# Relative attention and routed experts on one core: the Router's turns laid out by step, and the expert blocks in program order with their layer norm behind the gates

## The chip, the cores and the metric

The kernel runs on one core of a Trainium2 chip. The metric is the device time of one execution in microseconds (us); lower is better. All times below are in us unless they say ns. The engines of a core are PE (matmul; PEld is its weight load), DVE, ACT, POOL and SP; each works through its own queue of instructions in order, and they meet through semaphores.

## The reference

```python
x = x + layernorm(attention(layernorm(x)))     # 16 x 512 x 128, 16 heads of 8
x = x + layernorm(experts(layernorm(x)))

# attention: relative keys and values, distance clipped to +-128
scores = (q @ k.T + q . rel_k[idx]) / sqrt(8)
w      = softmax(scores)
out    = w @ v + w . rel_v[idx]

# experts: 16 experts, top 1, and a shared one
logits = x @ w_router.T
e      = argmax(logits);  s = sigmoid(logits[e])
gate, up = split((s * x) @ gate_up_proj[e])
out = (up * silu(gate)) @ down_proj[e] + (silu(x @ w_gate.T) * (x @ w_up.T)) @ w_down.T
```

All data is fp32, and `layernorm` has no weights.

## The kernel before

**Attention.** There are 16 batches of 512 tokens. A batch takes 16 steps, one for each (c, n): n is the quarter of the 512 tokens and c the 32-row piece within it, so that one step handles 32 queries of all heads, in four groups g. The loop `for i in range(total + 24)` runs over 256 steps and 24 more that drain the pipeline. I write k = i % 16 for the step within a batch and n = k % 4. A step issues, in this order: `scores` of step i (`ps<-km,qb` and then `ps<-relk,qr` on PE); the transposes `pt` of step i-1; `peak` (DVE's `nmax`) and `exps` (ACT); `attend` of step i-5 (`pa` on PE, then `od`, `oz` and `oT` on DVE); the other two transposes; then at most one piece of side work called `spare`: with n = 0 `sums_turn` (`prt`), with n = 1 `output` (`py`, then `y_sb` and its statistics on DVE), with k = 6, 7, 14 and 15 the projections of the next batch. After that come POOL's `keys_advance`, the Router's turns, and with n = 1 `expand` (POOL's `qb` and `qr` for step i+3).

All engines run in the order in which the attention loop writes their instructions: the class `InOrder` wraps each engine and keeps its program order. So an instruction that waits holds up everything behind it on its engine.

**The bank.** `bank()` (L218) gives a PSUM tile from the pool `ps_o`, which has one buffer. `attend`, every `spare` and three of the Router's turns use it one after another: each must wait until the one before has been copied out.

**The Router.** `route(b)` (L595) is a generator. It takes the batch's attention output through the residual and the second layer norm, computes the logits, picks the expert, gives each token a place in a list of 128-row blocks by expert, and writes the token's row `pay` to `rows` in DRAM with an indirect DMA. Its first part runs one batch late, from step 6 of the next batch on. It is cut into sixteen turns by `yield`:

| turn | what it does |
|---|---|
| 1 | `ry` power, normalisation of y and residual (POOL) |
| 2, 3 | statistics of two pieces each (DVE) |
| 4 | `l_ve` (DVE), power `l_rs`, `x2`, the mean and 1/std into `pay` (POOL) |
| 5 | bank: transposes `ptf` of x2, copied by ACT |
| 6 | bank: logits `pl`, copied by DVE |
| 7, 8 | maximum, one-hot `oh`, score (DVE, one exponential on ACT) |
| 9 | bank: `pr`, the places within an expert; eight additions on DVE |
| 10, 11, 12 | blocks, shifts, final places `at_i` (DVE) |
| 13 to 16 | one indirect DMA each (POOL) |

In all but the last batch a step with n > 0 gives each live Router one turn. In the last batch (`nxt is None`), a small table by k says how many.

**Experts.** The second stage works on 73 blocks of 128 rows (up to 79 are possible; the rest is under a branch). `fetch` loads a block's two expert weights `gu` and `dn` by its expert number, `turn_in` normalises the rows (DVE), scales them by the Router's score (ACT) and transposes both (`ptb`), `gates` makes gate and up for the shared and the chosen expert (`pg`, 16 matmul passes), the sigmoid and two products `g` and `h`, and `leave` makes the down projection (`po`), its layer norm, adds the row and writes it out by an indirect DMA. `run` (L953) issues `turn_in(i+1)`, `gates(i)`, `leave(i-1)`. Here the engines are not wrapped: the scheduler of the framework sets the order.

Of the kernel before, what the change touches and what calls it, by code (L numbers as in the profile page):

```python
# [17 lines left out]
P = 128  # L18
# [32 lines left out]
def relative_attention_then_moe(  # L51
# [31 lines left out]
    def stats(pool, mv, src, tag, eng):  # L83
        st = pool.tile([P, 6], F32, tag=f"{tag}_st", name=f"{tag}_st")
        eng.bn_stats(st, src)
        eng.bn_aggr(mv, st)  # L86

    def own_rows(group, dma):

        tc.declare_no_dep(dma.ins, group=group, reason="rows of their own")  # L90
        tc.add_to_no_dep_group(group, dma.ins)


    with ExitStack() as actx:
# [500 lines left out]
        def route(b, c0=0, c1=NC):  # L595
# [32 lines left out]
            for t in range(nc_):  # L628
                eng.tensor_scalar(
                    x2[:, t, :], pay[:, t, 0:D], mv[:, t, 0:1], rs1[:, t : t + 1], ALU.subtract, ALU.mult  # L630
                )
            pool.tensor_copy(pay[:, :, D : D + 1], mv[:, :, 0:1])
            pool.tensor_copy(pay[:, :, D + 1 : D + 2], rs1.unsqueeze(2))
            yield
            x2T = bp.tile([P, nc_ * P], F32, tag="x2T", name=f"x2T{nm}", bufs=1)
# [122 lines left out]
        for i in range(total + 24):  # L758
            b, c, n = at(i)
            k = i % 16  # L760
            last = i - 1 if 0 <= i - 1 < total else None
            old = i - 5 if 0 <= i - 5 < total else None
            live = i < total
            done = at(i - 9)[:2] if n == 1 and 0 <= i - 9 < total else None
            nxt = b + 1 if b + 1 < B else None

            spare = None
            if 0 < b < B and k == 6:
                routes[b - 1, 0] = route(b - 1)
# [12 lines left out]
            if nxt is not None:  # L782
                if k == 0 and b + 2 < B:
                    load_x(b + 2)
                if k in (6, 7, 14, 15):
                    f = {6: x_turn, 7: queries, 14: keys, 15: values}[k]
                    spare = lambda: f(nxt)

            if live:
                scores(b, c, n)  # L790
            if last is not None:
                T = {g: turn(*at(last), g) for g in ORDER[:2]}
            if live:
                for g in ORDER[:2]:
                    peak(b, c, n, g)
                    exps(b, c, n, g)
            if last is not None:
                dve.tensor_copy(*T[ORDER[0]])
                act.copy(*T[ORDER[1]])
            if live:  # L800
                for g in ORDER[2:]:
                    peak(b, c, n, g)
                    exps(b, c, n, g)
            if old is not None:
                attend(*at(old), done=done)()
            elif done is not None:
                join_places(bank([P, P], f"pj{b}"), *done)()
            if last is not None:
                T = {g: turn(*at(last), g) for g in ORDER[2:]}
            if spare is not None:  # L810
                leave = spare()
            if last is not None:
                dve.tensor_copy(*T[ORDER[2]])
                act.copy(*T[ORDER[3]])
            if spare is not None:
                leave()
            if nxt is not None and k in (0, 2):
# [12 lines left out]

            for r in sorted(routes):


                turns = (n > 0) if nxt is not None else {7: 2, 9: 0, 12: 0, 13: 2, 15: 2}.get(k, 1) if live else 1
                for _ in range(turns):
                    bank_user = next(routes[r], StopIteration)
                    if bank_user is StopIteration:
                        del routes[r]
                        break
                    elif bank_user is not None:  # L840
                        bank_user()()
            if n == 1 and i + 3 < total:
                expand(*at(i + 3)[:2])
# [4 lines left out]
    with ExitStack() as fctx:  # L848
        wp = fctx.enter_context(tc.tile_pool(name="ffn_w", bufs=1))
        xp = fctx.enter_context(tc.tile_pool(name="ffn_x", bufs=1))  # L850
        ep = fctx.enter_context(tc.tile_pool(name="ffn_e", bufs=4))
        fp = fctx.enter_context(tc.tile_pool(name="ffn", bufs=3))
        sp = fctx.enter_context(tc.tile_pool(name="ffn_small", bufs=4))
        ps_g = fctx.enter_context(tc.tile_pool(name="ps_g", bufs=2, space=PSUM))
        ps_x = fctx.enter_context(tc.tile_pool(name="ps_x", bufs=2, space=PSUM))
        ps_f = fctx.enter_context(tc.tile_pool(name="ps_f", bufs=2, space=PSUM))

        wgu = wp.tile([P, 2 * FF], F32, name="wgu")
        wd = wp.tile([P, 2, D], F32, name="wd")
# [41 lines left out]
            st["fetched"] = last.ins  # L901
            st[i] = {"x": x, "gu": gu, "dn": dn}

        def turn_in(i):

            x = st[i]["x"]
            x2 = fp.tile([P, 2, D], F32, tag="x2", name=f"x2b{i}")
            nc.vector.tensor_scalar(
                x2[:, 0, :], x[:, 0:D], x[:, D : D + 1], x[:, D + 1 : D + 2], ALU.subtract, ALU.mult
            )  # L910
            nc.scalar.mul(x2[:, 1, :], x2[:, 0, :], x[:, D + 2 : D + 3])  # L911
            pt = ps_x.tile([P, 2, P], F32, tag="x", name=f"ptb{i}")
            for k in range(2):
                nc.tensor.transpose(pt[:, k, :], x2[:, k, :], ident)
            xT = fp.tile([P, 2, P], F32, tag="xT", name=f"xTb{i}")
            nc.scalar.copy(xT, pt)
            st[i]["xT"] = xT

        def gates(i):

            xT = st[i]["xT"]
            pg = ps_g.tile([P, 2, 4, P], F32, tag="g", name=f"pg{i}")
            for k, w in enumerate((wgu, st[i]["gu"])):
                for c in range(4):
                    nc.tensor.matmul(pg[:, k, c, :], w[:, c * P : (c + 1) * P], xT[:, k, :], start=True, stop=True)
            g = fp.tile([P, 2, 2, P], F32, tag="g", name=f"g{i}")
            nc.scalar.activation(g, pg[:, :, 0:2, :], AF.Sigmoid)
            nc.vector.tensor_mul(g, g, pg[:, :, 0:2, :])
            h = fp.tile([P, 2, 2, P], F32, tag="h", name=f"h{i}")
            nc.vector.tensor_mul(h, g, pg[:, :, 2:4, :])  # L930
            st[i]["h"] = h

        def leave(i):

            s = st.pop(i)
            x, h = s["x"], s["h"]
            po = ps_f.tile([P, D], F32, tag="f", name=f"po{i}")
            for k, w in enumerate((wd, s["dn"])):
                for c in range(2):
                    nc.tensor.matmul(po, h[:, k, c, :], w[:, c, :], start=(k == c == 0), stop=(k == c == 1))  # L940
            mv = sp.tile([P, 1, 2], F32, tag="mvf", name=f"mvf{i}")
            stats(sp, mv[:, 0, :], po, "lf", nc.vector)
            rs = rstd_of(sp, mv, 1, "lf", nc.vector)
            f = fp.tile([P, D], F32, tag="f", name=f"f{i}")
            nc.vector.tensor_scalar(f, po, mv[:, 0, 0:1], rs, ALU.subtract, ALU.mult)
            nc.gpsimd.tensor_add(f, f, x[:, 0:D])
            to = ids_of[i]
            own_rows("out", nc.gpsimd.indirect_dma_start(  # L948
                out_rows, bass.IndirectOffsetOnAxis(ap=to, axis=0), f, None,
                bounds_check=B * S - 1, oob_is_err=False,  # L950
            ))

        def run(i0, i1):  # L953

            for i in range(i0, min(i0 + 3, i1)):
                fetch(i)
            turn_in(i0)
            for i in range(i0, i1 + 1):
                if i + 3 < i1:
                    fetch(i + 3)  # L960
                if i + 1 < i1:
                    turn_in(i + 1)
                if i < i1:
                    gates(i)
                if i > i0:
                    leave(i - 1)

        for c in range(2):
            fetch_rows(c)
# [37 lines left out]
```

## Time and profile before

| | us |
|---|---|
| median of 3 runs | 1970.33 (1968.71 to 1974.59) |
| the profiled execution | 1970.49 |
| its span, first to last instruction | 1968.8 |
| outside the span | 1.69 |
| start of the first and of the last of the 256 attention steps | 23.4 and 1681.1 of the span |
| start of the first and of the last of the 73 blocks' gates | 1732.9 and 1953.4 of the span |
| granted PE clock, mean | 0.990 (about 0.5 from 1709 to 1736 and from 1958 on) |

The profile comes from one execution. Line L47 stands for every wrapped instruction, because `InOrder` records them there; such rows are told apart by their tiles, written out<-in. A timeline row has the start within the span, the duration, the engine, the line, the operation, the tiles, the shapes, how many rows were merged, and in brackets the idle time of the engine ahead of it and what ended it. "issue" there means that the profile shows nothing that the engine waited for. In a row of busy times by stretch come the stretch, its length, the busy time and count of PE, PEld, DVE, ACT and POOL, the granted PE clock, the share in which the DMA engines were busy, and GB/s.

### The profile page before, as it was taken

How to read it: one execution, taken by the hardware profiler on the slowest of the kernel's cores; microseconds unless marked ns; L12 is line 12 of the kernel's file. 1: busy time of each engine (PE TensorE's matmuls, PEld its weight loads, DVE VectorE, ACT ScalarE, POOL GpSimd, SP SyncE). 2: the span in 40 equal slices, each digit the busy share in tenths (PEclk: the TensorE clock that was granted, in tenths of full speed). 3: DMA queues.
4: the chain of work that ended last, by engine and by line, in shares of the span. 5: the costliest groups of instructions: out<-in, count | busy, mean ns of one | idle time of the engine just before them, and what ended most of it. 6: DMA issues, size and time to landing. Idle time of an engine off the chain costs nothing. (4 is left out here: it accounts for less than half of the span.)

```text
span 1968.8 us, 87947 instructions
## 1 busy us (share of the span) xinstructions
PE 1885.2 (96%) x38254; PEld 1395.1 (71%) x38254; DVE 1532.0 (78%) x4051; ACT 1146.4 (58%) x2931; POOL 1009.3 (51%) x1405
## 2 busy tenths in 40 slices
PE   6999999999999999999999999999999999689997
PEld 3667767676776767767676767677676767579997
DVE  4777787878787878787887878787878787767776
ACT  3656666666666666656566666565666666234432
POOL 4245464545454554546454645454545544246666
PEclk9999999999999999999999999999999999889998
DMA  2412000000000000000000000000000000065553
GB/s 76 75 23 52 4 23 5 18 10 11 17 5 23 5 23 3 25 3 25 3 25 3 25 3 23 4 14 14 5 18 5 18 6 6 9 181 171 177 166 95
DMA packets 88326, 68.63 MB, mean 35 GB/s; under 512 B 26439, under 2 KB 74340, under 8 KB 87808
## 3 DMA queue, kind: packets, MB, share of 16 engines
q1 hardware_dynamic: 81248, 53.60, 10.2%
q0 software_dynamic: 4384, 8.57, 1.3%
q8 instruction: 301, 4.93, 1.0%
q10 hardware_dynamic: 2304, 0.80, 0.2%
q14 instruction: 89, 0.73, 0.1%
HBM read 44.79 MB, written 18.75 MB: 32 GB/s over the span
## 5 line engine op out<-in xcount | busy, mean ns | idle before, releaser
L47 ACT ACTIVATE w<-ps,nmax 128x512 f32<-128x512 f32 x1024 | 699.0, 693 | 589.2 <-DVE nmax L47 588.6
L47 DVE TENSOR_REDUCE nmax<-ps 128x1 f32<-128x512 f32 x1024 | 655.3, 682 | 265.3 <-PE ps L47 263.8
L47 PE MATMUL pt<-ident,w 128*128 128x128 f32 x4096 | 567.7, 280 | 6.8 <-DVE wT L47 2.7
L47 PEld LDWEIGHTS pt<-ident,w 128*128 128x128 f32 x4096 | 439.2, 141 | 135.8 <-issue 89.1
L47 DVE COPY wT<-pt 128x512 f32<-128x512 f32 x512 | 348.7, 681 | 0.7 <-PE pt L47 0.7
L47 ACT COPY wT<-pt 128x512 f32<-128x512 f32 x512 | 301.1, 588 | 27.7 <-PE pt L47 27.7
L47 PE MATMUL ps<-km,qb 32*128 32x512 f32 x2048 | 297.4, 643 | 3.5 <-POOL qb L47 3.5
L47 PEld LDWEIGHTS ps<-relk,qr 64*32 64x32 f32 x8192 | 124.3, 106 | 225.8 <-issue 183.3
L47 PE MATMUL pa<-wT,v 128*32 128x128 f32 x8192 | 276.7, 276 | 2.5 <-DVE oz L47 1.4
L47 PE MATMUL ps<-relk,qr 64*32 64x288 f32 (+4 forms) x8192 | 274.8, 377 | 0.0
L47 PEld LDWEIGHTS pa<-wT,v 128*32 128x32 f32 x8192 | 208.1, 109 | 45.3 <-issue 37.8
L47 ACT ACTIVATION_READ_ACCUMULATOR w<-ps,nmax 128x1 f32 x1024 | 211.5, 207 | 0.0
L47 POOL TENSOR_TENSOR Rh<-R,mh 128x512 f32<-128x512 f32 x64 | 66.5, 1039 | 278.6 <-ACT R L47 278.6
L47 PE MATMUL pa<-wT,relv 128*32 128x48 f32 (+1 forms) x12288 | 197.1, 210 | 7.4 <-issue 7.2
L47 PEld LDWEIGHTS pa<-wT,relv 128*32 128x32 f32 x12288 | 186.2, 110 | 9.9 <-issue 9.8
L47 POOL TENSOR_TENSOR qr<-qz,mq 128x1024 f32<-128x1024 f32 x64 | 137.5, 2149 | 0.0
L47 PEld LDWEIGHTS ps<-km,qb 32*128 32x128 f32 x2048 | 82.9, 183 | 59.7 <-issue 36.3
L47 POOL COPY km<-kT 128x32 f32<-128x32 f32 (+3 forms) x207 | 53.5, 263 | 134.4 <-ACT kT L47 134.3
L47 POOL TENSOR_SCALAR km<-kT,kend 128x32 f32<-128x32 f32 (+2 forms) x223 | 115.7, 520 | 2.2 <-PE ps L47 2.2
L911 ACT ACTIVATE x2b<-x2b,xc 128x128 f32<-128x128 f32 x73 | 29.0, 401 | 125.8 <-DVE mvf L86 59.6
L47 DVE TENSOR_TENSOR od<-pa,Rh 128x128 f32<-128x128 f32 x256 | 72.9, 285 | 33.7 <-PE pa L47 30.9
L47 DVE TENSOR_REDUCE oT<-od 128x32 f32<-128x128 f32 x256 | 94.8, 370 | 0.0
(161 smaller groups left out, 2300.6 us busy)
## 6 DMA issues: line engine op xcount, KB each, us to landing
gu<-_L_ffn_gate_up_proj_dram SPq DMA_DIRECT2D x73, 256.0 KB
dn<-in_L_ffn_down_proj_dram SPq DMA_DIRECT2D x73, 128.0 KB
rows<-zero SPq DMA_DIRECT2D x19, 266.0 KB
xc<-rows SPq DMA_DIRECT2D x8, 532.0 KB
x_sb<-in_L_attn_x_dram SPq DMA_DIRECT2D x64, 64.0 KB
qd<-qp SPq DMA_DIRECT2D x16, 256.0 KB
qz<-qd SPq DMA_DIRECT2D x248, 16.0 KB
relv<-vext SPq DMA_DIRECT2D x1, 1536.0 KB
```

The source lines that it names most:

```text
L47: return lambda *a, **k: self.tc.keep_in_program_order(op(*a, **k))
L911: nc.scalar.mul(x2[:, 1, :], x2[:, 0, :], x[:, D + 2 : D + 3])
```

## The change

It has two parts.

1. *Router.* For the Routers of batches 0 to 13, the turns come at fixed steps counted from step 6 of the next batch: at offsets 0 to 7 (steps 6 to 13), 12 to 17 (steps 2 to 7 of the batch after) and 19 to 21 (steps 9 to 11). The transposes of x2 are then in step 10, the logits in step 11 and the places in step 2. Before, they were in steps 11, 13 and 1. The Routers of the last two batches keep the table by k. In turn 4 the copy of the mean into `pay` becomes one DVE operation that writes -mean x 1/std instead.
2. *Experts.* All four engines are wrapped in `InOrder`. The row's normalisation goes from DVE to ACT (it uses the -mean x 1/std from `pay`) and is issued two blocks ahead (`norm`). The gate half of `pg` is made before the up half. The products come in their own part (`product`), the down projection two blocks behind the gates (`down_proj`), and the end four blocks behind: POOL makes mean x 1/std (`mr`), ACT makes `xb` = mr - x (`residual`), and DVE makes po x 1/std - xb in one operation (`leave`), where DVE normalised and POOL added before. The buffers of the weights go from 4 to 6, of the other SBUF tiles from 3 to 4, of `ps_x` from 2 to 1, of `ps_f` from 2 to 3.

```diff
-            pool.tensor_copy(pay[:, :, D : D + 1], mv[:, :, 0:1])
+            dve.scalar_tensor_tensor(
+                pay[:, :, D : D + 1], mv[:, :, 0:1], -1.0, rs1.unsqueeze(2), ALU.mult, ALU.mult
+            )
             pool.tensor_copy(pay[:, :, D + 1 : D + 2], rs1.unsqueeze(2))
...
-                turns = (n > 0) if nxt is not None else {7: 2, 9: 0, 12: 0, 13: 2, 15: 2}.get(k, 1) if live else 1
+                if r[0] < B - 2:
+                    turns = i - (r[0] + 1) * 16 - 6 in (0, 1, 2, 3, 4, 5, 6, 7, 12, 13, 14, 15, 16, 17, 19, 20, 21)
+                else:
+                    turns = {7: 2, 9: 0, 12: 0, 13: 2, 15: 2}.get(k, 1) if live else 1
...
-        ep = fctx.enter_context(tc.tile_pool(name="ffn_e", bufs=4))
-        fp = fctx.enter_context(tc.tile_pool(name="ffn", bufs=3))
+        ep = fctx.enter_context(tc.tile_pool(name="ffn_e", bufs=6))
+        fp = fctx.enter_context(tc.tile_pool(name="ffn", bufs=4))
...
+        pe, act, dve, pool = (InOrder(tc, e) for e in (nc.tensor, nc.scalar, nc.vector, nc.gpsimd))
...
+        def norm(i):
+            act.activation(x2[:, 0, :], x[:, 0:D], AF.Identity, bias=x[:, D : D + 1], scale=x[:, D + 1 : D + 2])
+            act.mul(x2[:, 1, :], x2[:, 0, :], x[:, D + 2 : D + 3])
...
+            pg = ps_g.tile([P, 2, 2, 2, P], F32, tag="g", name=f"pg{i}")
+            for u in range(2):
+                for k, w in enumerate((wgu, st[i]["gu"])):
+                    for c in range(2):
+                        a = u * FF + c * P
+                        pe.matmul(pg[:, u, k, c, :], w[:, a : a + P], xT[:, k, :], start=True, stop=True)
...
+            act.activation(g, pg[:, 0], AF.Sigmoid)
...
+        def product(i):
+            dve.tensor_mul(g, g, pg[:, 0])
+            dve.tensor_mul(h, g, pg[:, 1])
...
+        def down_proj(i):
+            stats(sp, mv[:, 0, :], po, "lf", dve)
+            rs = rstd_of(sp, mv, 1, "lf", dve, pool)
+            pool.tensor_mul(mr, mv[:, :, 0], rs)
...
+        def residual(i):
+            act.activation(xb, s["x"][:, 0:D], AF.Identity, bias=s["mr"], scale=-1.0)
...
+            dve.scalar_tensor_tensor(f, s["po"], s["rs"], s["xb"], ALU.mult, ALU.subtract)
...
+            norm(i0)
+            norm(i0 + 1)
             turn_in(i0)
-            for i in range(i0, i1 + 1):
+            for i in range(i0, i1 + 4):
                 if i + 3 < i1:
                     fetch(i + 3)
                 if i + 1 < i1:
                     turn_in(i + 1)
+                if i + 2 < i1:
+                    norm(i + 2)
+                if i0 <= i - 4 < i1:
+                    residual(i - 4)
                 if i < i1:
                     gates(i)
-                if i > i0:
-                    leave(i - 1)
+                if i0 <= i - 4 < i1:
+                    leave(i - 4)
+                if i < i1:
+                    product(i)
+                if i0 <= i - 2 < i1:
+                    down_proj(i - 2)
```

More of the change, by code (lines that the diff above doesn't have):

```diff
@@ L850, in relative_attention_then_moe @@
         xp = fctx.enter_context(tc.tile_pool(name="ffn_x", bufs=1))
-        ep = fctx.enter_context(tc.tile_pool(name="ffn_e", bufs=4))
-        fp = fctx.enter_context(tc.tile_pool(name="ffn", bufs=3))
+        ep = fctx.enter_context(tc.tile_pool(name="ffn_e", bufs=6))
+        fp = fctx.enter_context(tc.tile_pool(name="ffn", bufs=4))
         sp = fctx.enter_context(tc.tile_pool(name="ffn_small", bufs=4))
         ps_g = fctx.enter_context(tc.tile_pool(name="ps_g", bufs=2, space=PSUM))
-        ps_x = fctx.enter_context(tc.tile_pool(name="ps_x", bufs=2, space=PSUM))
-        ps_f = fctx.enter_context(tc.tile_pool(name="ps_f", bufs=2, space=PSUM))
+        ps_x = fctx.enter_context(tc.tile_pool(name="ps_x", bufs=1, space=PSUM))
+        ps_f = fctx.enter_context(tc.tile_pool(name="ps_f", bufs=3, space=PSUM))
+        pe, act, dve, pool = (InOrder(tc, e) for e in (nc.tensor, nc.scalar, nc.vector, nc.gpsimd))
         wgu = wp.tile([P, 2 * FF], F32, name="wgu")
@@ L902, in fetch, with turn_in @@
             st[i] = {"x": x, "gu": gu, "dn": dn}
-        def turn_in(i):
+        def norm(i):
             x = st[i]["x"]
             x2 = fp.tile([P, 2, D], F32, tag="x2", name=f"x2b{i}")
[L908 to L911, printed above, removed]
+            act.activation(x2[:, 0, :], x[:, 0:D], AF.Identity, bias=x[:, D : D + 1], scale=x[:, D + 1 : D + 2])
+            act.mul(x2[:, 1, :], x2[:, 0, :], x[:, D + 2 : D + 3])
+            st[i]["x2"] = x2
+        def turn_in(i):
             pt = ps_x.tile([P, 2, P], F32, tag="x", name=f"ptb{i}")
             for k in range(2):
-                nc.tensor.transpose(pt[:, k, :], x2[:, k, :], ident)
+                pe.transpose(pt[:, k, :], st[i]["x2"][:, k, :], ident)
             xT = fp.tile([P, 2, P], F32, tag="xT", name=f"xTb{i}")
-            nc.scalar.copy(xT, pt)
+            act.copy(xT, pt)
             st[i]["xT"] = xT
@@ L921, in gates @@
             xT = st[i]["xT"]
[L922 to L925, printed above, removed]
-            g = fp.tile([P, 2, 2, P], F32, tag="g", name=f"g{i}")
-            nc.scalar.activation(g, pg[:, :, 0:2, :], AF.Sigmoid)
-            nc.vector.tensor_mul(g, g, pg[:, :, 0:2, :])
+            pg = ps_g.tile([P, 2, 2, 2, P], F32, tag="g", name=f"pg{i}")
[4 more added lines that the diff above has]
+                        pe.matmul(pg[:, u, k, c, :], w[:, a : a + P], xT[:, k, :], start=True, stop=True)
+            g = fp.tile([P, 2, 2, P], F32, tag="g", name=f"g{i}")
+            act.activation(g, pg[:, 0], AF.Sigmoid)
+            st[i].update(pg=pg, g=g)
+        def product(i):
+            pg, g = st[i]["pg"], st[i]["g"]
+            dve.tensor_mul(g, g, pg[:, 0])
             h = fp.tile([P, 2, 2, P], F32, tag="h", name=f"h{i}")
-            nc.vector.tensor_mul(h, g, pg[:, :, 2:4, :])
+            dve.tensor_mul(h, g, pg[:, 1])
             st[i]["h"] = h
-        def leave(i):
-            s = st.pop(i)
-            x, h = s["x"], s["h"]
+        def down_proj(i):
+            s = st[i]
+            h = s["h"]
             po = ps_f.tile([P, D], F32, tag="f", name=f"po{i}")
@@ L939, in leave @@
                 for c in range(2):
-                    nc.tensor.matmul(po, h[:, k, c, :], w[:, c, :], start=(k == c == 0), stop=(k == c == 1))
+                    pe.matmul(po, h[:, k, c, :], w[:, c, :], start=(k == c == 0), stop=(k == c == 1))
             mv = sp.tile([P, 1, 2], F32, tag="mvf", name=f"mvf{i}")
-            stats(sp, mv[:, 0, :], po, "lf", nc.vector)
-            rs = rstd_of(sp, mv, 1, "lf", nc.vector)
-            f = fp.tile([P, D], F32, tag="f", name=f"f{i}")
[L945 to L949, printed above, removed]
+            stats(sp, mv[:, 0, :], po, "lf", dve)
+            s["po"] = po
+            rs = rstd_of(sp, mv, 1, "lf", dve, pool)
+            mr = sp.tile([P, 1], F32, tag="mr", name=f"mr{i}")
+            pool.tensor_mul(mr, mv[:, :, 0], rs)
+            s.update(rs=rs, mr=mr)
+        def residual(i):
+            s = st[i]
+            xb = fp.tile([P, D], F32, tag="xb", name=f"xb{i}")
+            act.activation(xb, s["x"][:, 0:D], AF.Identity, bias=s["mr"], scale=-1.0)
+            s["xb"] = xb
+        def leave(i):
+            s = st.pop(i)
+            f = fp.tile([P, D], F32, tag="f", name=f"f{i}")
+            dve.scalar_tensor_tensor(f, s["po"], s["rs"], s["xb"], ALU.mult, ALU.subtract)
+            own_rows("out", pool.indirect_dma_start(
+                out_rows, bass.IndirectOffsetOnAxis(ap=ids_of[i], axis=0), f, None,
                 bounds_check=B * S - 1, oob_is_err=False,
```

## The prediction, made before the result

> **What bounds the kernel now.** I read the page's busy times first, then the busy times by stretch, then the timeline of each engine; a share over the whole span hides that the attention and the expert stage wait for different things.
>
> ```profile
> PE 1885.2 (96%) x38254; PEld 1395.1 (71%) x38254; DVE 1532.0 (78%) x4051; ACT 1146.4 (58%) x2931; POOL 1009.3 (51%) x1405
> ```
> PE has work nearly all the time, so only what makes PE wait can be won, and work merely moved on PE wins nothing. In the timeline the score matmuls `ps<-km,qb` mark the start of each step (step k = i % 16 of a batch, n = k % 4). From one to the next I take each step's length. Batches 2 to 14 repeat within 0.1 us but for a few steps.
>
> The bank `ps_o` has one buffer. Here is PE in step 13 of batch 4 (n = 1), with `py` of `output` and then the Router's logits `pl`:
> ```profile
> 519.06 1.14 PE L47 MATMUL ps<-km,qb 32*128 32x512 f32 x8
> ...
> 525.41 0.39 PE L47 MATMUL py<-wo_h,oj 128*128 128x128 f32 x2
> 526.18 1.06 PE L47 MATMUL pl<-wr,x2T 128*128 128x16 f32 x8 [0.38 <-DVE y_sb L47]
> 527.18 1.14 PE L47 MATMUL ps<-km,qb 32*128 32x512 f32 x8
> ```
> The step lasts 8.12; the same step without a Router's user (step 1 of batch 15, 1591.53 to 1598.20) lasts 6.67. Of the 1.45, 1.00 is the logits' own work and 0.45 is waiting for the bank to be emptied by DVE. Next, steps 0 and 1 of the following batch:
> ```profile
> 540.29 1.14 PE L47 MATMUL ps<-km,qb 32*128 32x512 f32 x8
> ...
> 545.65 0.66 PE L47 MATMUL pt<-ident,w 128*128 128x128 f32 x4 [0.17 <-ACT wT L47]
> 546.51 0.63 PE L47 MATMUL prt<-ident,rb 128*128 128x128 f32 x4 [0.20 <-DVE oz L47]
> 547.07 1.14 PE L47 MATMUL ps<-km,qb 32*128 32x512 f32 x8
> ...
> 554.19 0.43 PE L47 MATMUL pr<-oh,before 128*128 128x64 f32 x2 [0.39 <-DVE y_sb L47]
> ```
> Step 0 lasts 6.78 and waits for a DVE that is late; in batch 1, with no Router ahead of it, it lasts 6.12. What makes DVE late is five small Router operations after step 15, two of them slow:
> ```profile
> 541.25 0.73 DVE L47 TENSOR_TENSOR oh<-oh,km 128x64 f32<-128x64 f32 x1
> 541.90 0.71 DVE L47 TENSOR_SCALAR pay<-km 128x4 int32<-128x4 f32 x1
> ```
> Step 1 lasts 7.71: 6.67, 0.59 of `pr` work and 0.45 of waiting.
>
> In the expert stage a block takes 26 matmuls. PE starts them 0.111 apart, so 2.90 is the least, and early blocks have it; most take 3.02:
> ```profile
> 1852.49 0.67 DVE L930 TENSOR_TENSOR h<-g,pg 128x512 f32<-128x512 f32 x1
> ```
> ```profile
> 1853.21 0.71 PE L940 MATMUL po<-wd,h 128*128 128x128 f32 x4
> ...
> 1856.26 0.71 PE L940 MATMUL po<-wd,h 128*128 128x128 f32 x4
> ```
> `h` ends at 1853.16 and the down projection starts at 1853.21: it waits each time, and one POOL stall of 2.91 before an indirect DMA (1894.50) passes through DVE's queue to PE in full, 2.34.
>
> **The change, part by part.** All in us, against the profiled execution's own 1970.49 (span 1968.8 and 1.69 around it; the median shown is 1970.33, so the sum holds for that as well).
>
> *Router, batches 0 to 13.* Of the sixteen turns of a batch, numbers 3 to 11 come at other steps (the two programs, listed engine by engine, show it); the first two and the last five stay. The logits go from step 13 to 11, where n = 3 has no other user: the 1.00 of work moves, the wait of 0.45 goes, 14 times: -6.3. The places go from step 1 to 2: -0.45 x 13 = -5.9 (the fourteenth is in the last batch, below). There the bank is empty (560.20) before PE gets there (560.45), so no new wait. The five operations after step 15 now follow step 13, where POOL has just ended `qr` (525.68); behind the 0.75 of `y_sb` they end 1.9 into step 14, whose first `nmax` can start at 1.94 (529.12 - 527.18). So step 0 falls to batch 1's 6.12, -0.66 x 13 = -8.6. The operations after step 2 shorten by 0.2 (eight that read PSUM, 0.97, for 1.23 of scans and subtractions): step 3 goes from 5.92 to 5.72 as in batch 1, -2.6; step 4 keeps its 0.32 over batch 1, step 5 has 1.71 of idle DVE for what follows step 4.
>
> *Last batch.* It now follows the same list for Router 13. Step 0, 8.26, falls to 6.12; the 0.59 of `pr` stays: -1.55. Step 5, 8.62, has two indirect DMAs (1619.10, 1620.61) beside PE's densest instructions and two "issue" gaps of 0.4 there and 0.27 behind them; the DMAs move to later steps: to 6.67, -1.95. One comes to step 9, which costs 0.45 in the other batches: +0.45. Together -3.05.
>
> *Transposes of x2, step 11 to 10.* Here n = 2 is tight. The work of 0.45 moves. The `rstd` and x2 move from step 10 to 9, with the new DVE product behind them: DVE's `l_ve` can run at 502.0, POOL's power takes 1.05 and x2 3.13:
> ```profile
> 507.91 1.05 POOL L47 TENSOR_TENSOR l_rs<-l_ve,mhalf 128x4 f32<-128x4 f32 x1 [4.08 <-DVE l_ve L47]
> 509.07 3.13 POOL L47 TENSOR_SCALAR x<-pay,mv,l_rs 128x128 f32<-128x128 f32 x4
> ```
> So the power ends at 503.3 and x2 at 506.6, just before PE is free for it (506.77). The new wait on DVE, for the power, has the four `nmax` of step 10 queued behind it, and ACT's exponentials behind them; PE has the first two ready only at 503.38, so with 0.17 for the product DVE loses 0.12. It then empties the bank at 507.0, and with 0.15 of handover (as `prt` at 546.51 after `oz`) PE starts at 507.13: +0.36 x 14 = +5.0. Bounds: 0 if DVE catches up, 1.0 if the product takes 0.78 (below).
>
> *POOL behind it.* `expand` (3.5) and the key advance (0.6) of step 9 are queued behind x2, and so end at 510.7 in place of 502.6; step 12 needs them at 512.9. The indirect DMA of step 10 moves from 502.76 to 510.9, and may meet PE's dense part in step 11. Such a meeting cost 0.4 in step 9; 0 or 0.4 x 13 = 5.2, I take the middle: +2.6.
>
> *The copy of the mean* leaves POOL (0.18): hidden, POOL was idle 4.08 there. In the tail the product runs twice in DVE's waits (0.65 for `pr`): nothing, at most +0.3. Attention: -6.3 - 5.9 - 8.6 - 2.6 - 3.05 + 5.0 + 2.6 = -18.9.
>
> *Experts.* `down_proj` comes two blocks behind the gates, so `h` is ready about 1.5 before PE asks. DVE loses the normalisation (0.49) and keeps 2 x 0.675 + 0.29 + 0.17 + 0.15 + 0.41 = 2.37; ACT gets three operations of 0.40 beside 0.58 and 0.37: 2.15; POOL loses the addition (0.43) and gains a product of 128x1 (about 0.18, as its smallest copy): 1.03 + 0.3 + 0.57 + 0.18 = 2.1. All stay under 2.90, and PE sets the pace; what `f` newly waits for, ACT's `xb`, was made possible two blocks earlier. The 72 periods last 220.5 (1732.88 to 1953.36); 72 x 2.90 = 208.8. I keep the first, slow-clocked block's 0.8 and 0.7 of small gaps: -10.2. POOL's stall is then covered by a two-block lag. With six weight buffers SP may fetch one block earlier; it issues a block in 1.8. At the start ACT does both halves of two blocks before it copies `xT` (+0.5), and the gate half needs the first `gu` after 4 matmuls, not 8 (+0.4): +0.9. At the end the last down projection follows the start of the last gates by 4.05 (gates 1.78, sigmoid 0.6, two products 1.37, handovers 0.3), not 4.82 (1953.36 to 1958.18), and PE stays fast (8 x 0.1), less one hop POOL to ACT: -1.6. Experts: -10.9.
>
> **Sum:** -18.9 - 10.9 = -29.8, that is 1940.7, say **1941**.
>
> **Rivals.** *DVE is held by POOL.* The slow rows above (0.73, 0.71) run beside POOL's `v` additions and end with them; alone such rows take 0.22 and 0.16. The new product reads two SBUF tiles just when POOL's x2 begins, 0.78 apiece: if x2 comes first, +0.6 x 14 = 8.4. The Router's additions after step 4 stand 0.2 ahead of POOL's `Rh` and `Rz` (1.04 each); if they fall behind, DVE is 1.1 late, of which 0.27 is idle time: +0.83 x 13 = 10.8. So 1949 with the first and 1960 with both. For the forecast speaks that after a power DVE begins 0.03 later (1961.52 + 0.58, then 1962.14) and POOL 0.11.
> The Trainium skill, "SBUF — State Buffer", section "Who interferes with whom", says that a DVE instruction with two SBUF inputs contends with a GpSimd instruction that reads SBUF, and that the second to issue blocks until the first finishes. The trace agrees: all of the `oh<-oh,km` beside the `v` additions take 0.73.
>
> *ACT becomes the experts' bound.* Five operations with a handover of 0.2 each would be 3.15 a block, above 3.02; its queue now has the sigmoid behind the norms. Then the 10.2 is lost: 1951. Against it: where work stands ready, ACT's rows follow without a gap (0.40 at 1850.67, the sigmoid at 1850.98).
>
> *The Router's moves cancel on PE* and only the experts gain: 1960.
>
> *Slower:* `expand` comes too late for step 12. It has 2.8 in hand after x2; PE then loses 14 us for each us beyond, and the gain is used up at 29.8 / 14 = 2.1 more, so from 4.9 late on. At 6 late it would be 1986. Only a POOL that starts the power that much later could do it, and it is free from 498.6.
>
> **Chances.** Forecast 0.58, DVE held 0.2, ACT 0.1, cancelled 0.06, slower 0.06. Below 1931 PE would need savings that I see in no row; the upper end takes in both held cases nearly: 1931 to 1959. A measurement tells 0.3% (6 us) from no change: faster by that 0.89, within it 0.05, slower 0.06.
>
> **What would show it.** Step 13 at 6.7, step 1 at 6.7, step 0 at 6.1, steps 10 and 11 at 6.6 and 6.5; the product at 0.17, not 0.8; `po<-wd,h` every 2.90 with no wait for `h`. Wrong if step 12 waits for `qr`, if step 5 exceeds 6.8, or if the sigmoid waits for ACT itself.

## The result and the profile after

| | before | after |
|---|---|---|
| median, same chip | 1970.47 | 1937.57 (1935.27 to 1939.64, 4 runs) |
| ratio, 95% interval | | 0.9835 (0.9823 to 0.9846) |
| the profiled execution | 1970.49 | 1937.03, span 1935.3 |
| first to last attention step | 1657.7 | 1632.8 |
| last attention step to first gates | 51.8 | 52.7 |
| first gates to last gates | 220.5 | 209.3 |
| last gates to the end of the span | 15.4 | 17.0 |

It is faster by 1.65%; the forecast was 1941. The profiled executions differ by 33.5, of which the attention gives 24.9 and the experts 8.7 (the first step starts 0.1 later). PE's busy time on the page falls by 17.6; the rest of the gain is idle time that went. ACT takes over work from DVE and POOL:

```profile
PE 1867.6 (96%) x38254; PEld 1391.1 (72%) x38254; DVE 1528.0 (79%) x3995; ACT 1208.7 (62%) x3077; POOL 992.1 (51%) x1388
```

I took the length of every step again, as the distance from one `ps<-km,qb` to the next. The medians of batches 2 to 13:

| step | 0 | 1 | 2 | 3 | 4 | 9 | 10 | 11 | 13 | all 16 |
|---|---|---|---|---|---|---|---|---|---|---|
| before | 6.78 | 7.71 | 5.82 | 5.92 | 6.26 | 7.12 | 5.82 | 5.97 | 8.12 | 104.27 |
| after | 6.15 | 6.67 | 6.22 | 5.71 | 6.13 | 7.13 | 6.43 | 6.74 | 6.67 | 102.58 |

The seven steps left out are equal to 0.01. In the timeline of PE after, here are the ends of step 13 (batch 4) and of step 2 (batch 5), where the Router's bank users stood and where the places stand now:

```profile
518.73 0.39 PE L47 MATMUL py<-wo_h,oj 128*128 128x128 f32 x2
519.04 1.14 PE L47 MATMUL ps<-km,qb 32*128 32x512 f32 x8
...
550.68 0.33 PE L47 MATMUL pr<-oh,before 128*128 128x64 f32 x2
550.85 0.39 PE L47 MATMUL pr<-oh,every 128*128 128x64 f32 x2
551.16 0.71 PE L47 MATMUL ps<-km,qb 32*128 32x512 f32 x4
```

After `py` the next step follows at once, with no Router's user between. `pr` in step 2 starts without a wait (no bracket). DVE after step 13 runs the operations that were slow before at their short times:

```profile
520.13 0.23 DVE L47 TENSOR_TENSOR oh<-oh,km 128x64 f32<-128x64 f32 x1
520.27 0.17 DVE L47 TENSOR_SCALAR pay<-km 128x4 int32<-128x4 f32 x1
```

In step 11 the logits do not wait for the bank, but PE stands in the dense part ahead of them. An indirect DMA on POOL begins at 605.19, and at 606.17 PE waits for "issue":

```profile
606.34 0.63 PE L47 MATMUL pa<-wT,relv 128*32 128x48 f32 x33 [0.17 <-issue]
...
607.84 0.96 PE L47 MATMUL pl<-wr,x2T 128*128 128x16 f32 x8
608.73 1.14 PE L47 MATMUL ps<-km,qb 32*128 32x512 f32 x8
```

In the expert stage the first two distances between gates are 4.15 and 2.48; all that follow are 2.90 but the last (2.68). `h` of one block is done at 1853.02 (1852.33 + 0.69), and the down projection that follows at 1853.68 is that of the block before, so PE never waits for `h`:

```profile
1852.33 0.69 DVE L47 TENSOR_TENSOR h<-g,pg 128x512 f32<-128x512 f32 x1
```
```profile
1853.68 0.61 PE L47 MATMUL po<-wd,h 128*128 128x128 f32 x4
...
1856.58 0.61 PE L47 MATMUL po<-wd,h 128*128 128x128 f32 x4
```

Two places got worse. The first is step 9 of the last batch: 9.40 after, 6.67 before, and step 10 behind it 7.29 for 6.26. The timelines of POOL, DVE and PE there:

```profile
1614.83 1.04 POOL L47 TENSOR_TENSOR Rh<-R,mh 128x512 f32<-128x512 f32 x1 [4.25 <-ACT R L47]
1615.82 1.04 POOL L47 TENSOR_TENSOR Rz<-R,mz 128x512 f32<-128x512 f32 x1
...
1617.19 1.05 POOL L47 TENSOR_TENSOR l_rs<-l_ve,mhalf 128x4 f32<-128x4 f32 x1
```
```profile
1618.27 0.17 DVE L47 SCALAR_TENSOR_TENSOR pay<-mv,l_rs 128x4 f32<-128x4 f32 x1 [4.12 <-POOL l_rs L47]
```
```profile
1620.29 0.66 PE L47 MATMUL pt<-ident,w 128*128 128x128 f32 x4 [1.30 <-DVE wT L47]
...
1623.29 2.09 PE L47 MATMUL ps<-km,qb 32*128 32x512 f32 x8
```

The small product stands in DVE's queue ahead of the step's `nmax` and waits for POOL's power, and the power waits behind `Rh` and `Rz`. DVE begins the `nmax` at 1618.35 only, and PE stands idle for 1.30 behind it. Then its granted clock falls to 0.5 for 3.41, so that the next eight score matmuls take 2.09 for 1.14. The second place is the end, taken up below.

### The profile page after: what moved, and what is told of

It reads as the page before. It is cut to its first block, busy times and chain, and to the rows that moved or that the text cites. A ratio compares the mean times of both kernels' runs of the same rounds, so it can differ in the third digit from the quotient of the medians.

```text
span 1935.3 us, 88211 instructions
## 1 busy us (share of the span) xinstructions
PE 1867.6 (96%) x38254; PEld 1391.1 (72%) x38254; DVE 1528.0 (79%) x3995; ACT 1208.7 (62%) x3077; POOL 992.1 (51%) x1388
## 5 line engine op out<-in xcount | busy, mean ns | idle before, releaser
L47 PE MATMUL pt<-ident,w 128*128 128x128 f32 x4096 | 561.5, 280 | 4.6 <-DVE wT L47 4.0
L47 POOL DMA_INDIRECT out_dram<-f,to x73 | 75.9, 1040 | 46.1 <-issue 32.3
L47 POOL COPY rb<-rt 128x512 f32<-128x512 f32 x64 | 39.4, 616 | 114.9 <-DVE rt L47 114.7
```

Of the source, the lines that this page charges most:

```text
L47: return lambda *a, **k: self.tc.keep_in_program_order(op(*a, **k))
```

## The experiments

The runs were made on further chips, each beside the kernel before: chip B (before 1961.20), C (1975.62) and D (1961.9). A is the chip of the result (1970.47). Times of different chips cannot be compared; ratios and steps can. The changed kernel itself ran on A and C alone.

### One part at a time

e1 has the old expert stage, only with the norm's two operations fitted to the new content of `pay`; e2 has the old turns.

```diff
# e2, from the changed kernel
-                if r[0] < B - 2:
-                    turns = i - (r[0] + 1) * 16 - 6 in (0, 1, 2, 3, 4, 5, 6, 7, 12, ...)
-                else:
-                    turns = {7: 2, 9: 0, 12: 0, 13: 2, 15: 2}.get(k, 1) if live else 1
+                turns = (n > 0) if nxt is not None else {7: 2, 9: 0, ...}.get(k, 1) if live else 1
```

> The Router's part alone (the turns by step and the product on DVE), with the expert stage as before; only the two operations of the expert stage's normalisation are swapped, because the row now holds -mean/std. Theory: the steps of the changed kernel's trace are all of the attention's gain, and they do not depend on the experts: first to last step falls from 1657.7 to 1632.8, so 1970.5 - 24.9 = 1945.6, with the last batch's step 9 at 9.4 and step 11 of the steady batches at 6.74. Rival: the shares are as in the forecast, and the attention alone gives 18.9: 1951.6.

> The experts' part alone: the changed kernel with the Router's turns as before. Theory: the expert stage gives 8.7 (start +1.0, 72 periods -11.2, end +1.5), less what DVE's product at the old places costs: 1961.8, with the product waiting for POOL's power and the last batch's steps as before but for that. Batch 0, in which no Router runs, is 102.2 as before if its 2.8 came from the Router's order of instructions, and 99.4 if it came from anything else of the change. Rival: forecast's shares, 10.9: 1959.6.

Chip B. e1: 1933.39, ratio 0.9858 (0.9843 to 0.9874), -27.8. e2: 1954.15, ratio 0.9961 (0.9948 to 0.9975), -7.1. The split is that of the trace: the Router's part does most of it. Its 27.8 is more than the 24.9 of the trace. Two differences between the steps go that way: step 11 is 6.38 in e1, without the gap that it has on chip A (6.74), and the last batch is 96.44 in place of 97.87. e2 has the expert stage of the changed kernel (209.4 from first to last gates, end 17.0), and its step 9 of the last batch is 8.88, so the product alone brings that wait, 2.2. In e1 that step is 8.88 too, at the full clock; on chip A, with the fallen clock, it is 9.40.

Two things were not expected. Batch 0, where no Router runs, is 99.75 in e1 and 99.95 in e2, which has before's order of turns; over all runs here it lies between 99.0 and 104.6. So the 2.8 that batch 0 gave in the result is scatter, and no effect of the change. And step 9 is 6.67 in both, in all of batches 1 to 14 but one each, where its median is 7.12 on chip A. Its indirect DMA is there, at the same 3.54 of the step, and PE does not stop for it.

### The product later, for all and for one

```diff
# e3 (e8: the same for b == B - 2 alone)
-            dve.scalar_tensor_tensor(pay[:, :, D : D + 1], mv[:, :, 0:1], -1.0, ...)
             pool.tensor_copy(pay[:, :, D + 1 : D + 2], rs1.unsqueeze(2))
             yield
+            dve.scalar_tensor_tensor(pay[:, :, D : D + 1], mv[:, :, 0:1], -1.0, ...)
             x2T = ...
```

> The changed kernel with the product -mean/std one turn later in the program, in the turn that turns x2. Theory: only in the last batch did DVE wait for it (4.12 at 1618.27, because POOL's power stands behind Rh and Rz there): step 9 falls from 9.40 to 6.67 and step 10 from 7.29 to 6.26, TensorE's clock stays at 1.0 there, the steady batches do not move: 1937.6 - 3.8 = 1933.8. Rival: the transposes or POOL's order make that wait anyway, and the step stays over 9: 1937.6.

e3 on chip B: 1930.20, ratio 0.9841 (0.9828 to 0.9855). The last batch did as expected (step 9 6.67, step 10 6.26). The steady batches did not stay: step 10 fell from 6.43 to 6.26, but step 11 is 7.23, where e1 on the same chip has 6.38, so a batch is 0.67 longer. DVE and POOL in step 11 of e3:

```profile
600.23 2.76 DVE L47 SCALAR_TENSOR_TENSOR pay<-mv,l_rs 128x4 f32<-128x4 f32 x1
```
```profile
599.49 1.32 POOL L47 TENSOR_TENSOR qb<-qp,mh 128x512 f32<-128x512 f32 x1
600.78 2.14 POOL L47 TENSOR_TENSOR qr<-qz,mq 128x1024 f32<-128x1024 f32 x1
```

An operation on 4 numbers a partition lasts 2.76: it starts beside `qb` and ends with `qr`, at 602.92. Thirteen of the products are held in this way (2.75 to 2.77). That is the rival "DVE is held by POOL" of the prediction, at another place. In the changed kernel the product takes 0.17 each time: there it stands directly behind the power, and starts 0.07 ahead of POOL's x2 (597.73 and 597.80). The rule cited in the prediction (the Trainium skill, "SBUF — State Buffer", section "Who interferes with whom") has the second to issue blocked until the first finishes; the thirteen agree in part: DVE is blocked, but beyond `qb`, which issued first, until `qr` ends. In batch 1 of the same run the product was let go with `qb` (0.54), and in e5, below, each of two DVE operations ends with one POOL operation. What decides between the two cases was not found.

> The changed kernel with the product -mean/std one turn later for batch 14's Router alone, the one that runs in the last batch; all others stay where the power of POOL has just ended. Theory: DVE's wait in the last batch's step 9 goes (9.40 or 8.9 to 6.67) and no product is held, as 2.76 each was with all of them later: 3.3 less than the changed kernel beside it (2.2 from step 9, up to 1.1 from step 10 where the clock fell). Rival: as in the run with all products later, the product meets POOL's qb and qr and gives 2 back.

e8 on chip C: 1937.49, ratio 0.9822 (0.9803 to 0.9840), beside the changed kernel itself at 1941.97 (below). Step 9 of the last batch is 6.67 for 9.39, step 10 6.86 for 7.29: 3.2 less, where 3.3 was expected. The steps show this, not the times: the intervals of the two ratios overlap, and batch 0 with its scatter alone differs by 3.7 between the profiled executions (100.9 for 104.6). No product is held (0.155 to 0.169 each).

### The bank and DVE's small operations

```diff
# e4                                               # e5
-  ... 6, 7, 12, 13, ...                           -  ... 6, 7, 12, 13, ...
+  ... 6, 7, 11, 13, ...                           +  ... 6, 9, 12, 13, ...
```

> The changed kernel with one bank user put back: the places behind step 1, where y_sb holds the only bank, in place of step 2. Theory: step 1 goes from 6.67 to 7.71 and step 2 from 6.22 to 5.82: 0.64 a batch, 13 or 14 times, +8.6: 1946.2. Of the 0.64, 0.45 is the wait for the bank and 0.19 is pr's own work, which is longer when PE starts it from a standstill. Rival: the bank costs nothing, and the gain of steps 0 to 4 comes from DVE's small operations alone: within 1 of 1937.6.

> The changed kernel with the five small operations that make the router's key (oh, km, pay) put back from the end of step 13 to the end of step 15, where POOL adds v. Theory: oh<-oh,km and the one after it take 0.73 and 0.71 there, because POOL's v additions hold them, DVE is late for step 0, and step 0 goes from 6.14 to 6.78: 0.64 x 13 = +8.3 on the changed kernel's time of the same chip (1938 to 1942 on two chips, 1928 on the third). Rival: step 0 was late for the logits' wait in step 13, which is gone; then step 0 stays at 6.14 and the time does not move.

e4 on chip B: 1932.31, ratio 0.9846 (0.9833 to 0.9860). Step 1 is 7.71 and step 2 5.82, as expected to the hundredth. PE waits for the bank again, in each of the 14 batches:

```profile
547.13 0.43 PE L47 MATMUL pr<-oh,before 128*128 128x64 f32 x2 [0.38 <-DVE y_sb L47]
```

Step 4 falls to 6.01, which I had not expected, so that a batch is 0.53 longer than in e1 (102.26 for 101.73) and not 0.64. So the bank has its price, and the rival has fallen. The time of e4 says nothing more, as the changed kernel did not run on chip B.

e5 on chip D: 1932.79, ratio 0.9857 (0.9842 to 0.9872). Step 0 is 6.77 or 6.78 in each of batches 2 to 15, and the median of no other step moves against e9 on the same chip. DVE and POOL of e5 at the end of step 15:

```profile
531.78 0.74 DVE L47 TENSOR_TENSOR oh<-oh,km 128x64 f32<-128x64 f32 x1
532.44 0.71 DVE L47 TENSOR_SCALAR pay<-km 128x4 int32<-128x4 f32 x1
```
```profile
531.70 0.74 POOL L47 TENSOR_TENSOR v<-v,v_lo 128x256 f32<-128x256 f32 x1 [4.98 <-DVE v L47]
532.39 0.73 POOL L47 TENSOR_TENSOR v<-v,v_hi 128x256 f32<-128x256 f32 x1
```

Each is as long as the POOL operation beside it. So step 0's 0.64 comes from the five operations behind step 15, of which these two are held, and the rival (the logits' wait in step 13) has fallen: step 13 is 6.67 in e5. No run puts the logits themselves back. That they lengthened step 13 by 1.45 is read from the trace alone: without them it is 6.67, after and in batch 15 before.

### What carries the expert stage

The forecast put the period of 2.90 down to the down projection's second block of lag. e6 takes one block away from everything behind the gates, e9 only from the residual and the end, e7 leaves the order to the scheduler.

```diff
# e6: down_proj(i - 2) -> (i - 1), residual(i - 4) and leave(i - 4) -> (i - 3)
# e9:                              residual(i - 4) and leave(i - 4) -> (i - 3)
# e7
-        pe, act, dve, pool = (InOrder(tc, e) for e in (nc.tensor, nc.scalar, nc.vector, nc.gpsimd))
+        pe, act, dve, pool = nc.tensor, nc.scalar, nc.vector, nc.gpsimd
```

> The changed kernel once more, beside the runs below, because the kernel before took 1970.5 on one chip and 1961.2 on another. Theory: what differs between chips are the gaps of 0.45 in step 9 (both kernels) and 0.36 in step 11 (changed kernel only) beside an indirect DMA; where they are absent, step 9 is 6.67, step 11 is 6.38, the kernel takes some 10 less (1927 to 1929), and the ratio is a little better than 0.9835, by 4.7 of 1961, so 0.981. Rival: the gaps belong to the program, they come back here, and the ratio is 0.9835 on every chip.

> The changed kernel with the down projection one block behind the gates in place of two, and the residual and the leaving three in place of four. Theory of the forecast: the second block of lag is what hides h, so the period goes back from 2.90 to about 3.02, and the kernel loses 0.12 x 72 = 8.6. Rival, from the changed kernel's trace: h is ready 4.03 after its gates start, since the sigmoid now begins after half of the matmuls and DVE has lost the normalisation, and PE asks for it at 4.68; so the period stays at 2.90, and the tail, which POOL drains at 2.52 a block, gets one block shorter: 1 to 2.5 less than the changed kernel beside it.

> The changed kernel with the experts' engines taken without the fixed program order, so that the scheduler places the operations; PE's order stays the same, DVE gets f ahead of lf_ve and the statistics between the two products, ACT gets the norms in another order. Theory: the lag of two blocks is enough, and the time is within 2 of the changed kernel beside it. Rival: f ahead of lf_ve waits for POOL as before, the chain h to PE is late again, the period is 3.0 and the time 7 to 10 more.

> The changed kernel with residual and leaving three blocks behind the gates in place of four, the down projection still two behind: one block between mr and the residual that reads it, in place of two. Theory: what holds the period at 2.90 is that distance. With one block, ACT's xb stands in front of the sigmoid and waits for mr; the circle sigmoid 0.60, g and h 1.4, statistics and lf_ve 0.6, POOL's power and mr 1.0, xb 0.4 and some 0.1 of handovers is 4.1 long and takes a block's time: +1.2 x 72 = +86 on the changed kernel's time. Rival: mr of the block comes early enough, as only POOL's part of 1.1 lies between lf_ve and xb, and the period stays at 2.90 with a tail one block shorter: -2.5.

| | chip | median | ratio, 95% | typical period | first to last gates | from there to the end |
|---|---|---|---|---|---|---|
| changed again | C | 1941.97 | 0.9834 (0.9817 to 0.9850) | 2.90 | 209.3 | 17.0 |
| e6 | C | 1939.34 | 0.9824 (0.9809 to 0.9840) | 2.90 | 210.2 | 14.5 |
| e7 | C | 1954.74 | 0.9897 (0.9879 to 0.9915) | 3.02 | 219.5 | 19.0 |
| e9 | D | 1996.82 | 1.0172 (1.0156 to 1.0188) | 3.90 | 277.3 | 21.5 |

The changed kernel repeats its ratio on chip C, and its steps 9 and 11 (7.14 and 6.76) as on A. e6 shows that the second block of lag is not what hides `h`: the period stays. What it does hide, wholly, is one stall of POOL, 3.19 ahead of the 50th block's DMA, which all versions have (2.91 before). In the changed kernel it costs nothing, in e6 one period is 3.46, before it was 5.50. POOL in e6:

```profile
1870.39 1.09 POOL L47 DMA_INDIRECT out_dram<-f,to  x1 [3.19 <-ACT xTb L47]
```

e7 has the same lags in the program and the same matmuls in the same order, but for one early down projection, and is back at before's 3.02. The rival had the period right, and its reason only in part: `f` does stand ahead of `lf_ve`, but it waits for ACT's `xb`, and PE has no wait for `h` (none from 1760 to 1860). ACT, DVE, POOL and PE in e7:

```profile
1851.92 0.40 ACT L969 ACTIVATE xb<-xc,mr 128x128 f32<-128x128 f32 x1 [1.05 <-POOL mr L962]
1852.23 0.35 ACT L925 COPY xTb<-ptb 128x256 f32<-128x256 f32 x1
```
```profile
1852.39 0.32 DVE L976 SCALAR_TENSOR_TENSOR f<-po,lf_rs,xb 128x128 f32<-128x128 f32 x1
1852.63 0.15 DVE L78 TENSOR_SCALAR lf_ve<-mvf 128x1 f32<-128x1 f32 x1
```
```profile
1853.00 1.07 POOL L977 DMA_INDIRECT out_dram<-f,to  x1 [0.95 <-ACT x2b L915]
1854.10 0.58 POOL L80 TENSOR_TENSOR lf_rs<-lf_ve,mhalf 128x1 f32<-128x1 f32 x1
1854.76 0.19 POOL L962 TENSOR_TENSOR mr<-mvf,lf_rs 128x1 f32<-128x1 f32 x1
```
```profile
1852.64 0.44 PE L923 MATMUL ptb<-ident,x2b 128*128 128x128 f32 x2
```

In e7 `xb` runs as soon as `mr` is there, so `xb`, `f`, the DMA, the power and `mr` follow one another, and the next `xb` is at 1854.99: a circle of 3.07 (3.02 in the block before) that each block goes through once. PE seems to meet it at `ptb`, for which `ps_x` now has one buffer: ACT's copy `xTb` behind `xb` empties it at 1852.58, and the next `ptb` starts at 1852.64. e9 makes a circle by hand, and puts the products into it. ACT in e9:

```profile
1853.79 0.40 ACT L47 ACTIVATE xb<-xc,mr 128x128 f32<-128x128 f32 x1 [1.93 <-POOL mr L47]
1854.10 0.58 ACT L47 ACTIVATE g<-pg 128x512 f32<-128x512 f32 x1
```

`xb` stands ahead of the sigmoid in the queue and waits for `mr` in each block, then come the sigmoid, `g`, `h`, the statistics and POOL. I had added up 4.1; it takes 3.90, so the periods bring +68.0 and the end +4.5, less than the 86 expected. So the program order matters, and in it the distance of two blocks between `mr` and the `xb` that reads it. e6 kept that distance.

What lets one block of lag be enough is that `h` is ready 4.03 after the start of its gates (1848.99), where it was 4.83 before (1848.33 to 1853.16). Of the 0.80, the sigmoid gives 0.66. ACT before, then ACT and PE after:

```profile
1850.67 0.40 ACT L911 ACTIVATE x2b<-x2b,xc 128x128 f32<-128x128 f32 x1 [1.72 <-DVE h L930]
1850.98 0.58 ACT L927 ACTIVATE g<-pg 128x512 f32<-128x512 f32 x1
```
```profile
1850.98 0.60 ACT L47 ACTIVATE g<-pg 128x512 f32<-128x512 f32 x1 [0.30 <-PE pg L47]
```
```profile
1850.33 0.61 PE L47 MATMUL pg<-xTb,gu 128*128 128x128 f32 x4
```

Before, the sigmoid stands behind `x2b`, which waits for DVE's normalisation (it ends at 1850.57). After, it starts 0.04 behind the last of all sixteen `pg` matmuls, in every block, and 0.93 behind the last of the gate half. So making the gate half first does not help it, and the expectation of e6 is wrong in that. No run puts the normalisation back alone.

The end is POOL's. Once PE has nothing more to do, at 1924.46, POOL in the changed kernel still has two powers and four DMAs, one behind the other, 2.52 for a block:

```profile
1925.58 0.58 POOL L47 TENSOR_TENSOR lf_rs<-lf_ve,mhalf 128x1 f32<-128x1 f32 x1
...
1927.03 1.03 POOL L47 DMA_INDIRECT out_dram<-f,to  x1 [0.60 <-ACT xb L47]
1928.10 0.58 POOL L47 TENSOR_TENSOR lf_rs<-lf_ve,mhalf 128x1 f32<-128x1 f32 x1
```

One block less in e6 is worth the 2.5 that were expected in this stretch (14.5 for 17.0). The ratios of the two kernels do not tell it; their intervals overlap.

### Both places mended, and the DMAs moved

```diff
# e10: the lags of e6, and
-            dve.scalar_tensor_tensor(pay[:, :, D : D + 1], mv[:, :, 0:1], -1.0, ...)
+            pool.tensor_scalar(pay[:, :, D : D + 1], mv[:, :, 0:1], -1.0, None, ALU.mult)
+            pool.tensor_mul(pay[:, :, D : D + 1], pay[:, :, D : D + 1], rs1.unsqueeze(2))
# e11: e10, and the third and fourth DMA of a Router at offset 23, behind expand of step 13;
#      the power of turn 4 at offset 2, its x2 at offset 3
```

> The changed kernel with two things mended: -mean/std is made by two small POOL operations behind x2 (0.2 each) in every batch, so DVE waits for no power and shares no port; and the back end one block earlier (down projection one, residual and leaving three behind the gates). Theory: last batch -3.3 (step 9 from 9.40 to 6.67, step 10 from 7.29 to about 6.7), tail -2.5, steady batches 0: 5.8 less than the changed kernel, a ratio of 0.9805 on a chip like the first. Rival: POOL's 0.2 more pushes expand and the key advance, step 11 or 12 waits for it, and 13 x 0.2 is given back.

> As the run with the product on POOL, and in the steady batches the third and fourth indirect DMA move from steps 9 and 10 to behind expand in step 13, where they fall on the start of step 14, and the power moves to step 8's end so that x2 is done before step 10. Theory: on a chip that has the gaps, step 9 falls from 7.13 to 6.67, step 11 from 6.74 to 6.38, and step 10 stays at 6.43 or falls to 6.35: -0.8 x 13 = -10.5 against the run with the product on POOL (0 to -1 on a chip without gaps). Rivals: a DMA costs PE its gap wherever it falls, and step 14 grows by what 9 and 11 lose; or step 10 waits for x2 for as long as step 9 gets shorter, as in batch 1 (6.67 and 6.90), and only 0.36 x 13 = 4.7 is won.

e10 on chip D: 1918.75, ratio 0.9776 (0.9763 to 0.9789), by its ratio the fastest version together with e11. It is lower than the 0.9805 expected by 0.0029: on D the gap in step 11 is missing (4.7), and step 10 gives 2.2 that I had not counted, together 0.0035. Step 9 of the last batch is 6.67, the end 14.7, and step 10 of the steady batches 6.26 for 6.43, so 0.17 of it was DVE's product. Nothing waits for the longer POOL chain: steps 11 and 12 are 6.38 and 6.15. e11: 1918.10, ratio 0.9774 (0.9761 to 0.9788), no difference. On chip D there were no gaps in steps 9 and 11 to begin with (6.67 and 6.38 in e5, e9 and e10), so whether the move is worth its 10 on a chip that has them stays open.

## Why the prediction was right, and where it was not

The sign, the size and the split came out: -29.8 forecast, -33.5 in the profiled executions. But the sum has errors of both signs that cancel in part, and 2.8 of the gain is the scatter of batch 0; that it came so near is partly luck. By its own terms:

| term | forecast | measured on chip A |
|---|---|---|
| logits' wait for the bank | -6.3 | (-1.45 + 0.88) x 14 = -8.0 |
| places' wait | -5.9 | (-1.04 + 0.40) x 13 = -8.3 |
| step 0 | -8.6 | -0.63 x 13 = -8.2 |
| step 3; step 4 | -2.6; 0 | -2.7; -1.7 |
| transposes of x2 in step 10 | +5.0 | (-0.47 + 0.44 + 0.17) x 13 = +1.8 |
| the DMA beside step 11 | +2.6 | 0.36 x 13 = +4.7 (0 on B and D) |
| last batch | -3.05 | 97.84 to 97.87: 0.0 |
| batch 0 | 0 | -2.8, scatter |
| experts: start, periods, end | +0.9, -10.2, -1.6 | +1.0, -11.2, +1.5 |

No step 11 here is without a bank user. I estimate it at 5.50: its last `pt` starts 4.48 into it, and step 10 before, which has no user, ends 1.02 after the start of its last `pt`. The 0.88 is step 11 without a gap (6.38) less 5.50, the 0.47 is 5.97 less 5.50, and the 0.44 is step 10 of e10 (6.26) less 5.82.

*Bank and DVE.* The mechanisms hold: e4 and e5 put single moves back and get before's step lengths. The work of the two users was mis-sized: `pr` costs 0.40 where PE goes into it without a stop, not the 0.59 that it takes from a standstill in step 1, and the logits by the estimate 0.88, not 1.00.

*Step 10.* The step that failed is "DVE loses 0.12" and "empties the bank at 507.0". DVE in step 10, which starts at 595.56:

```profile
597.73 0.17 DVE L47 SCALAR_TENSOR_TENSOR pay<-mv,l_rs 128x4 f32<-128x4 f32 x1 [1.17 <-POOL l_rs L47]
597.80 1.29 DVE L47 TENSOR_REDUCE nmax<-ps 128x1 f32<-128x512 f32 x2
```

I added the product's whole 0.17, but the `nmax` starts 0.07 after it. So DVE begins the `nmax` 2.24 into the step, where it was 2.27 before (503.38), and loses nothing against that; without the product, in e10, it begins at 1.95 (the median). The wait of PE is 0.17 and not 0.36, by e10.

*Last batch.* The step that failed is "One comes to step 9, which costs 0.45 in the other batches": I priced the DMA there, and worked out the new wait for the power only for the steady batches, where POOL is idle ahead of it. In the last batch the same turn comes at step 8, and the power falls behind `Rh` and `Rz`. e2 shows that the product alone does this (8.88), e8 that without it step 9 is 6.67. Steps 0, 2 and 5 give -2.1, +0.4 and -2.0 there, close to the forecast, and steps 9 and 10 take 2.7 and 1.0. For step 10 I had followed the new wait to the `nmax` queued behind it, and did not do so for the one batch with another table.

*Experts.* The saving was right and its reason wrong: "`down_proj` comes two blocks behind the gates, so `h` is ready about 1.5 before PE asks". It is ready 3.56 before (1853.02, and 1856.58 for its down projection). e6 has one block and the same period; e7 has two and loses it; e9 names the pair that needs the distance. The last term failed in its sign: PE's end was priced, with the last down projection 4.05 behind the gates, and it came at 4.97, because it waits for the PSUM buffer that `f` of three blocks before gives back:

```profile
1923.30 0.71 PE L47 MATMUL po<-wd,h 128*128 128x128 f32 x4 [1.24 <-DVE f L47]
```

More than that, POOL's queue of 2.52 a block ends the kernel. I had its work at 2.1, with 0.3 ahead of each DMA where POOL takes 0.60.

*Rivals.* "DVE is held by POOL" did not happen in the change: no product is held, and step 5 stays at 6.67. e3 shows that it does happen one turn later. "ACT becomes the bound" did not happen: ACT's sigmoid waits for PE's `pg` (0.30 in each block), not for ACT. That the Router's moves cancel on PE is refuted by e1, which gains without the experts. "Slower" did not happen: step 12 is 6.15 as before.

## What to carry to other kernels

A wait that is added to an in-order queue has to be followed in every variant of the schedule, the last round and the drain above all; the steady state hides it. A DVE instruction of 4 numbers a partition with two operands took 2.76 beside two POOL instructions and 0.17 elsewhere, so its place is worth more thought than its size. When a chain runs through three engines, look for the circle that each block goes through once: here the distance in blocks between the writer `mr` and the reader `xb` set the period (2.90 with two, 3.90 with one), while the lag of the down projection could be one block shorter.

## What the runs showed of the hardware

- The "issue" gaps of PE beside an indirect DMA go with the chip in these runs, whatever the kernel; whether the chip itself makes them, or where a program lies on it, is not shown. On A and C step 9 has a median of 7.12 to 7.15 in the steady batches of all kernels traced there, on B and D 6.67, with the DMA at the same 3.54 of the step (e11 has none there). The kernel before takes 1970.5 and 1975.6 on the first two and 1961.2 and 1961.9 on the others; 13 x 0.45 = 5.9 of the difference would be these gaps, an estimate, since the kernel before was traced on A alone. What makes them was not found.
- Of nine traced executions with the wait in step 9 of the last batch, two show PE's granted clock at 0.5 for 3.41 behind it (both of the changed kernel; step 9 is 9.40 on A and 9.39 on C), and seven do not (8.87 to 8.89). PE had stood idle for 1.3 at a stretch and 1.9 in all.
- Batch 0, in which no Router runs, took 99.0 to 104.6 from run to run, mainly in its steps 1 and 10 to 12.
